# Attention block on one core: row sums taken on TensorE from three running sums, one step less lag, and the last two query blocks kept in the x buffers

## The chip, the cores and the metric

The kernel runs on one core of one Trainium2 chip. The time is the device time of one launch in microseconds (us), the median of several runs. A profile of one execution gives the start and the duration of every instruction. TensorE does matmuls, VectorE (DVE) elementwise work and statistics, ScalarE (ACT) the exponentials, GpSimd (POOL) elementwise work in SBUF, and SyncE (SP) issues most transfers.

## What is computed

```python
# x: (4, 512, 48, 48) float32, so 4 images of 512 channels and t = 2304 positions
hn  = group_norm(x, 32 groups) * gn_scale + gn_bias
qkv = einsum('oc,bchw->bohw', qkv_w, hn) + qkv_b            # fp32 weights
q, k, v = qkv.reshape(b, 3, 8 heads, 64, t).astype(float16)
w   = softmax(einsum('bhct,bhcs->bhts', q * s, k * s))      # s = 1 / 64 ** 0.25
a   = einsum('bhts,bhcs->bhct', w, v)
out = x + einsum('oc,bchw->bohw', proj_w, a) + proj_b
```

The softmax has no maximum subtracted in this path: the exponentials are summed, and the result is divided by the sum. A check of the sums' size sets a flag, and another path would run if it failed.

## The kernel before

Heads go in pairs, one on partitions 0 to 63 and one on 64 to 127; 4 images x 4 pairs are 16 pairs g. Queries go in blocks of 512, 512, 512, 512 and 256 (j = 0 to 4). The 18 groups of 128 keys of a block are worked in steps of three score tiles (BURST); a block of 512 has 6 steps, the block of 256 has 3, so there are 27 x 16 = 432 steps. A step is a unit `u = (g, j, k, last)`.

```python
BURST = 3
BEHIND = 2          # values run this many steps behind the scores

ps_s = ...tile_pool(name="ps_s", bufs=3, space=PSUM)    # score tiles
ps_av = ...tile_pool(name="ps_av", bufs=1, space=PSUM)  # values, and the sums, in turn
ps_w = ...tile_pool(name="ps_w", bufs=1, space=PSUM)    # projections
ppool = ...tile_pool(name="ppool", bufs=3)              # exponentials p of a step

def scores(u):
    pt = ppool.tile([P, BURST, 2, QB], F16, tag="p")
    for r in range(BURST):
        ps = ps_s.tile([P, 2, QB], F32, tag="ps")
        # ... matmuls of both heads into ps ...
        nc.scalar.activation(pt[:, r], ps, AF.Exp)

def values(u):
    # ... av += v^T p for both heads; at the last step of a block:
    if last:
        avx[g, j] = work.tile([P, QB], F32, tag="avx")
        nc.vector.tensor_copy(avx[g, j][:, :n], av[0][:, :n])

def direct(g, j):
    return g == NG - 1 and j >= NQ - 2      # the last two blocks of the last pair

def add(u):
    # ... the first two steps make acc, later ones are added to it (128 x 3072, fp16)
    t = acc[g, j][0]
    nc.vector.tensor_tensor(t, before, pt, ALU.add)
    if last:
        for r in range(1, BURST):           # the join of the three parts
            nc.vector.tensor_tensor(t[:, 0], t[:, 0], t[:, r], ALU.add)
        acc[g, j] = [t[:, :1]]

def add_up(g, j):
    sl = ps_av.tile([P, QB], F32, tag="av")
    steps = [(t, r, a) for t in acc.pop((g, j))
             for r in range(t.shape[1]) for a in range(per)]   # per = 1, or 2 for 256 queries
    for i, (t, r, a) in enumerate(steps):
        for h in range(2):
            lo = h * D
            nc.tensor.matmul(sl[lo : lo + D, :n], ones16, t[:, r, h, a * n : (a + 1) * n],
                             start=(i == 0), stop=(i == len(steps) - 1))
    # ... slx: sl copied to SBUF by VectorE, then transposed by DMA, inverted,
    #     broadcast by DMA (ib), and multiplied into avx by GpSimd, giving att
    # ... for a direct block: reciprocal and product on VectorE instead
```

The output projection of a block converts att to fp32r (`a`), multiplies with a high and a low part of the weights, and adds bias and residual. The residual `r` is loaded from HBM into one of three buffers and becomes the output tile, which is stored from there:

```python
def residual(b, j, m):
    xt = work.tile([P, QB], F32, tag="res", bufs=3)[:, :n]
    nc.sync.dma_start(xt, x[b, bass.ts(m, P), o : o + n])

def att32(b, j, pairs=range(NC)):
    # a buffer of one, "a32", for all four pairs (the very last block: a p buffer)
    for c in pairs:
        engine = nc.vector if direct(b * NPAIR + c, j) else nc.gpsimd
        engine.tensor_copy(at32[b, j][:, c, :n], atts[b * NPAIR + c][:, o : o + n])

def proj_end(b, j, m, ps):
    nc.vector.scalar_tensor_tensor(xt, ps[:, :n], bproj[:, m : m + 1], xt, ALU.add, ALU.add)
    nc.sync.dma_start(out[b, bass.ts(m, P), o : o + n], xt)
```

The loop puts pieces of other work (the next pairs' projections, the next image's statistics, the last image's output projection) between scores and values, by `fill`:

```python
for n in range(end):
    summed = stream[n - BEHIND - 1][:2] if ended(n - BEHIND - 1) else None
    if summed:
        add_up(*summed)
    wanted(stream[n][0], n)
    scores(stream[n])
    if n > 0:
        add(stream[n - 1])
    if summed:
        fill(n)
    if n >= BEHIND:
        values(stream[n - BEHIND])
    # ... check_sums, invert, divide of an ended block, one and two steps later
    if not summed:
        fill(n)
add(stream[-1])
for u in stream[-BEHIND:]:
    values(u)
check_sums(NG - 1, NQ - 2)
att32(B - 1, NQ - 1, range(NC - 1))
add_up(NG - 1, NQ - 1)
att32(B - 1, NQ - 1, (NC - 1,))
while beside:
    issue(end)
# ... the projection of the very last block
```

Of the kernel before, what the change touches and what calls it, by code (L numbers as in the profile page):

```python
# [11 lines left out]
F32 = mybir.dt.float32  # L12
F32R = mybir.dt.float32r
F16 = mybir.dt.float16
I32 = mybir.dt.int32
AF = mybir.ActivationFunctionType
ALU = mybir.AluOpType
# [12 lines left out]
NT = T // P  # L30
SCALE = float(np.float16(1.0 / math.sqrt(math.sqrt(D))))
BURST = 3
BEHIND = 2
LAG = 2


# [430 lines left out]
def fast_path(  # L467
# [169 lines left out]
    def piece(us, run, first=False, last=False, gap=0):  # L637
        return [us, run, first, last, gap, 0, NG]
# [93 lines left out]

    def residual(b, j, m):
        o, n = QBLOCKS[j]
        xt = work.tile([P, QB], F32, tag="res", bufs=3, name=f"r_{b}_{j}_{m}")[:, :n]
        nc.sync.dma_start(xt, x[b, bass.ts(m, P), o : o + n])
        res[b, j, m] = xt

    def att32(b, j, pairs=range(NC)):
        o, n = QBLOCKS[j]  # L740
        if (b, j) == (B - 1, NQ - 1):

            if (b, j) not in at32:
                t = ppool.tile([P, BURST, 2, QB], F16, tag="p", name="a32_last")
                t = t.rearrange("p r h n -> p (r h n)")[:, : 2 * NC * n]
                at32[b, j] = t.bitcast(F32R).rearrange("p (c n) -> p c n", c=NC)
        else:
            at32[b, j] = work.tile(
                [P, NC, QB], F32R, tag="a32", bufs=1, name=f"a32_{b}_{j}"
            )  # L750
        for c in pairs:
            engine = nc.vector if direct(b * NPAIR + c, j) else nc.gpsimd
            engine.tensor_copy(  # L753
                at32[b, j][:, c, :n], atts[b * NPAIR + c][:, o : o + n]
            )

    def proj_chain(b, j, m, ps):
        n = QBLOCKS[j][1]
        for c in range(NC):
            for i, w in enumerate((whi, wlo)):  # L760
                nc.tensor.matmul(  # L761
                    ps[:, :n],
                    w[:, c, bass.ts(m, P)],
                    at32[b, j][:, c, :n],
                    start=(c == 0 and i == 0),
                    stop=(c == NC - 1 and i == 1),
                )
# [9 lines left out]
    def proj_pieces(b, j):  # L777


        n = QBLOCKS[j][1]  # L780

        def run(chunk):
            bank = chain_bank(f"pr_{b}_{j}_{chunk[0]}")
            places = [bank[:, i * n : (i + 1) * n] for i in range(len(chunk))]
            for m, ps in zip(chunk, places):
                proj_chain(b, j, m, ps)
            for m, ps in zip(chunk, places):
                proj_end(b, j, m, ps)

        def ahead(k):  # L790
            if k < NQ * NC:
                residual(b, k // NC, k % NC)

        convert = [piece(0.0, lambda: att32(b, j))]
        chains = []
        per = QB // n
        for m in range(0, NC, per):
            chunk = range(m, m + per)
            loads = [j * NC + i + 2 for i in chunk]
            if (j, m) == (0, 0):  # L800
                loads = [0, 1] + loads
            chains.append(
                [piece(0.0, lambda i=i: ahead(i)) for i in loads]
                + [piece(QB / 290.0, lambda chunk=chunk: run(chunk), True, True)]
            )
        return convert, chains
# [61 lines left out]
    def direct(g, j):  # L868

        return g == NG - 1 and j >= NQ - 2  # L870

    def add(u):

        g, j, k, last = u
        pt = pts[u]
        if k == 0:
            acc[g, j] = [pt]
            return
        if last and direct(g, j):
            acc[g, j].append(pt)  # L880
            return
        before = acc[g, j][0]
        if k == 1:
            acc[g, j] = [
                work.tile(
                    [P, BURST, 2, QB], F16, tag="acc", bufs=1, name=f"acc_{g}_{j}"
                )
            ]
        t = acc[g, j][0]
        nc.vector.tensor_tensor(t, before, pt, ALU.add)  # L890
        if last:
            for r in range(1, BURST):
                nc.vector.tensor_tensor(t[:, 0], t[:, 0], t[:, r], ALU.add)  # L893
            acc[g, j] = [t[:, :1]]

    def add_up(g, j):

        o, n = QBLOCKS[j]
        per = QB // n
        sl = ps_av.tile([P, QB], F32, tag="av", name=f"sl_{g}_{j}")  # L900
        steps = [
            (t, r, a)
            for t in acc.pop((g, j))
            for r in range(t.shape[1])
            for a in range(per)
        ]
        for i, (t, r, a) in enumerate(steps):
            for h in range(2):
                lo = h * D
                nc.tensor.matmul(  # L910
                    sl[lo : lo + D, :n],
                    ones16,
                    t[:, r, h, a * n : (a + 1) * n],
                    start=(i == 0),
                    stop=(i == len(steps) - 1),
                )

        def rows():
            sx = work.tile([P, QB], F32, tag="rows", name=f"slx_{g}_{j}")
            nc.vector.tensor_copy(sx[:, :n], sl[:, :n])  # L920

            sm = small.tile([P, 2, QB // P], F32, tag="sums", name=f"sums_{g}_{j}")
            for h in range(2):
                nc.sync.dma_start(sm[:, h, : n // P], sx[h * D : h * D + 1, :n])
            sums[g, j] = sm
            return sx

        if direct(g, j):
            source = rows() if n == QB else sl
            inv = work.tile([P, QB], F32, tag="rows", name=f"inv_{g}_{j}")  # L930
            nc.vector.reciprocal(inv[:, :n], source[:, :n])
            nc.vector.tensor_tensor(
                atts[g][:, o : o + n], avx.pop((g, j))[:, :n], inv[:, :n], ALU.mult
            )
            if source is sl:
                rows()
        else:
            rows()

    def check_sums(g, j):  # L940
        n = QBLOCKS[j][1]
        sm = sums[g, j][:, :, : n // P]
        ok = fine[:, :, : n // P]
        for op, limit in ((ALU.is_ge, SUM_MIN), (ALU.is_le, SUM_MAX)):
            t = small.tile([P, 2, QB // P], F32, tag="in", name=f"in_{g}_{j}")
            t = t[:, :, : n // P]
            nc.gpsimd.tensor_scalar(t, sm, limit, None, op)  # L947
            nc.gpsimd.tensor_tensor(ok, ok, t, ALU.mult)
# [32 lines left out]
    def put_run(run, *args, gap=0, us=0.0):  # L981

        put([piece(us, lambda: run(*args), us > 0, us > 0, gap)])
# [15 lines left out]

    def ready(b, j):  # L1000

        return BEHIND + (2 if direct((b + 1) * NPAIR - 1, j) else 5)

    def put_convert(b, j):
        end = ends[((b + 1) * NPAIR - 1) * NQ + j]
        put(projs[b, j][0], end + ready(b, j))

    def put_proj(b, j, *which):

        end = ends[((b + 1) * NPAIR - 1) * NQ + j]  # L1010
        for i in which or range(len(projs[b, j][1])):
            put(projs[b, j][1][i], end + ready(b, j) + 1)

    for b in range(B):
# [13 lines left out]
        if b == B - 1:  # L1028
            put_convert(old, 0)
            put_qk(g + 3, 1)  # L1030
            for j in range(NQ):
                put_qk(g + 3, 0, (j,))
                put_proj(old, j)
                if j + 1 < NQ:
                    put_convert(old, j + 1)
            for j in range(NQ - 1):
                put_convert(b, j)
                put_proj(b, j)
            continue

        for j in range(NQ):
# [87 lines left out]
    ended = lambda n: 0 <= n < len(stream) and stream[n][3]  # L1129
    end = len(stream)  # L1130
    for n in range(end):
        summed = stream[n - BEHIND - 1][:2] if ended(n - BEHIND - 1) else None
        if summed:
            add_up(*summed)
        wanted(stream[n][0], n)
        scores(stream[n])
        if n > 0:
            add(stream[n - 1])
        if summed:

            fill(n)
        if n >= BEHIND:
            values(stream[n - BEHIND])
        if ended(n - BEHIND - 2):
            check_sums(*stream[n - BEHIND - 2][:2])
            if not direct(*stream[n - BEHIND - 2][:2]):
                invert(*stream[n - BEHIND - 2][:2])
        if ended(n - BEHIND - 3):
            divide(*stream[n - BEHIND - 3][:2])
        if not summed:  # L1150
            fill(n)
    alone[0] = True
    add(stream[-1])
    for u in stream[-BEHIND:]:
        values(u)
    check_sums(NG - 1, NQ - 2)
    att32(B - 1, NQ - 1, range(NC - 1))
    add_up(NG - 1, NQ - 1)
    att32(B - 1, NQ - 1, (NC - 1,))
    while beside:  # L1160
# [66 lines left out]
```

## Time and profile before

| | |
|---|---|
| time, median of 3 | 1688.02 us (1685.82 to 1689.22) |
| span of the profiled run | 1687.5 us, mean granted TensorE clock 0.987 |
| exponentials, ScalarE | 1296 of 128x1024, mean 1027 ns, 1231.3 us |
| adds of p to the running sums, VectorE | 350 of 128x3072, means 1805 and 1756 ns, 627.6 us |
| transfers of a 128x512 residual / output | 2.9 us / 2.8 us from issue to landing |
| HBM | 47 GB/s over the span |

A line of the profile begins with the line of the kernel and the engine. L893 is the join, L910 the matmuls of the sums, L866 the copy of the values to avx, L890 the adds to the running sums, L832 the scores, L857 the values, L761 the output projection, L772 its eviction, L590 the statistics and L839 the exponentials. PE is TensorE's matmul side and PEld its weight loads. "idle before" is the time that the engine stood still just before, with what ended it behind an arrow.

### The profile page before, as it was taken

How to read it: one execution, taken by the hardware profiler on the slowest of the kernel's cores; microseconds unless marked ns; L12 is line 12 of the kernel's file. 1: busy time of each engine (PE TensorE's matmuls, PEld its weight loads, DVE VectorE, ACT ScalarE, POOL GpSimd, SP SyncE). 2: the span in 40 equal slices, each digit the busy share in tenths (PEclk: the TensorE clock that was granted, in tenths of full speed). 3: DMA queues.
4: the chain of work that ended last, by engine and by line, in shares of the span. 5: the costliest groups of instructions: out<-in, count | busy, mean ns of one | idle time of the engine just before them, and what ended most of it. 6: DMA issues, size and time to landing. Idle time of an engine off the chain costs nothing.

```text
span 1687.5 us, 28311 instructions
## 1 busy us (share of the span) xinstructions
PE 1602.8 (95%) x11504; PEld 702.1 (42%) x11504; DVE 1134.2 (67%) x1280; ACT 1232.6 (73%) x1297; POOL 363.3 (22%) x497
## 2 busy tenths in 40 slices
PE   4999999799999999999999999998999999999796
PEld 1533443244333443445333344444533334444344
DVE  5257666876666667777666666876766666676764
ACT  0078787777787787677777877766777888877980
POOL 1002212112211211232221121133221121223331
PEclk9999999899999999999999999999999999999998
DMA  6001002200000013430100001442110000034243
GB/s 206 1 15 29 13 15 66 70 14 17 14 11 14 17 27 95 128 98 17 48 14 11 14 17 41 102 126 79 22 43 11 14 17 14 14 92 116 58 113 109
DMA packets 93772, 81.84 MB, mean 49 GB/s; under 512 B 50880, under 2 KB 58944, under 8 KB 93632
## 3 DMA queue, kind: packets, MB, share of 16 engines
q1 hardware_dynamic: 91488, 76.51, 17.2%
q10 hardware_dynamic: 1968, 3.41, 0.6%
q8 instruction: 92, 1.51, 0.4%
q14 instruction: 48, 0.39, 0.1%
q0 software_dynamic: 176, 0.02, 0.0%
HBM read 60.44 MB, written 19.16 MB: 47 GB/s over the span
## 4 chain that ended last, share of the span: by engine, by line
PE 86%; DVE 6%; DMA 3%; ACT 3%; issue 2%; POOL 0%; SPq 0%; DVEq 0%; POOLq 0%; ACTq 0%
PE pqk L673 29%; PE ps L832 17%; PE av L857 17%; PE pv L713 14%; PE pr L761 7%; ACT p L839 3%; DVE acc L890 2%; PE sl L910 1%; DVE st L590 1%; DMA out_dram<-r 1%; DMA x<-x_dram 1%; DVE acc L893 1%; DMA r<-x_dram 1%; DVE x L629 0%; DVE r L772 0%
## 5 line engine op out<-in xcount | busy, mean ns | idle before, releaser
L839 ACT ACTIVATE p<-ps 128x1024 f16<-128x1024 f32 x1296 | 1231.3, 1027 | 401.7 <-PE ps L832 400.1
L673 PE MATMUL pqk<-x,wqkv 128*64 128x512 f32 (+1 forms) x2560 | 539.2, 553 | 8.6 <-DVE x L629 4.2
L890 DVE TENSOR_TENSOR acc<-acc,p 128x3072 f16<-128x3072 f16 x270 | 487.2, 1805 | 74.5 <-ACT p L839 74.0
L832 PE MATMUL ps<-q,k 64*128 64x512 f16 (+1 forms) x2880 | 365.7, 361 | 15.6 <-ACT p L839 15.2
L857 PE MATMUL av<-p,v 128*64 128x512 f16 (+1 forms) x2880 | 363.7, 366 | 0.1
L673 PEld LDWEIGHTS pqk<-x,wqkv 128*64 128x64 f32 x2560 | 175.7, 137 | 249.0 <-issue 181.0
L947 POOL TENSOR_SCALAR in<-sums 128x8 f32<-128x8 f32 (+1 forms) x160 | 117.4, 734 | 736.0 <-DMA sums<-slx 728.7
L713 PE MATMUL pv<-wqkv,x 128*64 128x256 f32 x2304 | 267.9, 380 | 2.5 <-DVE r L772 1.5
L832 PEld LDWEIGHTS <-k 64*128 64x128 f16 x2880 | 107.6, 94 | 295.6 <-issue 249.8
L857 PEld LDWEIGHTS <-v 128*64 128x64 f16 x2880 | 132.0, 109 | 212.5 <-issue 169.3
L969 POOL TENSOR_TENSOR att<-avx,ib 128x512 f16<-128x512 f32 (+1 forms) x78 | 125.7, 1612 | 432.1 <-DMA ib<-row 384.6
L713 PEld LDWEIGHTS pv<-wqkv,x 128*64 128x64 f32 x2304 | 159.8, 137 | 96.0 <-DVE v L721 6.4
L890 DVE TENSOR_TENSOR acc<-p,p 128x3072 f16<-128x3072 f16 x80 | 140.4, 1756 | 0.3 <-ACT p L839 0.3
L761 PE MATMUL pr<-a,whi 128*128 128x512 f32 (+1 forms) x304 | 122.8, 410 | 5.6 <-POOL a L753 3.2
L682 DVE TENSOR_SCALAR q<-pqk,bqkv 128x512 f16<-128x512 f32 (+1 forms) x80 | 55.7, 697 | 100.5 <-PE pqk L673 100.2
L721 DVE TENSOR_TENSOR v<-pv,bv 128x512 f16<-128x512 f32 x72 | 49.7, 691 | 103.3 <-PE pv L713 103.2
L893 DVE TENSOR_TENSOR acc<-acc 128x1024 f16<-128x1024 f16 x156 | 112.2, 719 | 5.3
L761 PE MATMUL pr<-a,wlo 128*128 128x512 f32 (+1 forms) x304 | 115.1, 385 | 0.0
L682 DVE TENSOR_SCALAR k<-pqk,bqkv 128x512 f16<-128x512 f32 (+1 forms) x80 | 55.7, 696 | 84.0 <-PE pqk L673 83.9
L772 DVE SCALAR_TENSOR_TENSOR r<-pr,bproj,r 128x512 f32<-128x512 f32 (+1 forms) x80 | 55.3, 695 | 70.3 <-PE pr L761 57.4
L866 DVE COPY avx<-av 128x512 f32<-128x512 f32 (+1 forms) x80 | 50.9, 636 | 57.4 <-PE av L857 57.3
L753 POOL CAST a<-att 128x512 fp32r<-128x512 f16 (+1 forms) x75 | 60.9, 845 | 98.2 <-PE pr L761 97.8
(57 smaller groups left out, 420.8 us busy)
## 6 DMA issues: line engine op xcount, KB each, us to landing
r<-x_dram SPq DMA_DIRECT2D x64, 256.0 KB, 2.9
out_dram<-r SPq DMA_DIRECT2D x64, 256.0 KB, 2.8
ib<-row SPq DMA_DIRECT2D x126, 128.0 KB, 3.0
x<-x_dram SPq DMA_DIRECT2D x56, 256.0 KB, 3.7
x<-x_dram ACTq DMA_DIRECT2D x8, 256.0 KB, 6.8
wqkv<-qkv_wT_dram SPq DMA_DIRECT2D x2, 1024.0 KB, 8.3
sums<-slx SPq DMA_DIRECT2D x128, 2.0 KB, 2.1
r<-x_dram SPq DMA_DIRECT2D x16, 128.0 KB, 2.1
```

What stands on the lines that cost most here:

```text
L673: nc.tensor.matmul(pw[0][lo : lo + D, :n], wqkv[:, c, w0 + lo : w0 + lo + D], hn[b, c, j], start=(c == 0), stop=(c == NC - 1),)
L682: nc.vector.tensor_scalar(qk[g][part][:, o : o + n], pw[0][:, :n], bqkv[:, col : col + 1], SCALE, ALU.add, ALU.mult,)
L713: nc.tensor.matmul(pw[0][lo : lo + D, a, :], hn[b, c, i * P // QB][:, at + lo : at + lo + D], wqkv[:, c, 2 * C + half * C // 2 :][:, : C / ...
L753: engine.tensor_copy(at32[b, j][:, c, :n], atts[b * NPAIR + c][:, o : o + n])
L761: nc.tensor.matmul(ps[:, :n], w[:, c, bass.ts(m, P)], at32[b, j][:, c, :n], start=(c == 0 and i == 0), stop=(c == NC - 1 and i == 1),)
L832: nc.tensor.matmul(ps[:, h, a * n : (a + 1) * n], kt[rows, bass.ts(i, P)], qt[rows, o : o + n], start=True, stop=True,)
L839: nc.scalar.activation(pt[:, r], ps, AF.Exp)
L857: nc.tensor.matmul(av[0][lo : lo + D, :n], vv[b, pr // 2][:, i, pr % 2 * P + lo : pr % 2 * P + lo + D], pt[:, r, h, a * n : (a + 1) * n], ...
L890: nc.vector.tensor_tensor(t, before, pt, ALU.add)
L893: nc.vector.tensor_tensor(t[:, 0], t[:, 0], t[:, r], ALU.add)
L947: nc.gpsimd.tensor_scalar(t, sm, limit, None, op)
L969: nc.gpsimd.tensor_tensor(atts[g][:, o : o + n], avx.pop((g, j))[:, :n], ib[:, :n], ALU.mult)
```

## The change

Three things change together. The join of the three parts of a running sum on VectorE is left out, and the sum matmuls on TensorE take all three parts. Values run one step behind the scores instead of two, and all that follows an ended block comes a step earlier. And the residuals and the converted att of the last two query blocks go to the x buffers, which nobody reads any more in the last pair; they are loaded and converted (three of four pairs) during the last pair, so that the end need not wait for three residual buffers in turn.

```diff
-BEHIND = 2
...
     def residual(b, j, m):
         o, n = QBLOCKS[j]
-        xt = work.tile([P, QB], F32, tag="res", bufs=3, name=f"r_{b}_{j}_{m}")[:, :n]
+        if at_end(b, j):
+
+            tag = f"x{m}_{j - NQ + 2}"
+            xt = xpool.tile([P, QB], F32, tag=tag, name=f"r_{b}_{j}_{m}")[:, :n]
+        else:
+            xt = work.tile([P, QB], F32, tag="res", bufs=3, name=f"r_{b}_{j}_{m}")
+            xt = xt[:, :n]
         nc.sync.dma_start(xt, x[b, bass.ts(m, P), o : o + n])
...
+    def at_end(b, j):
+
+        return b == B - 1 and j >= NQ - 2
...
-        if (b, j) == (B - 1, NQ - 1):
-            (cut: a p buffer for the last block; one a32 buffer for all pairs else)
+        if (b, j) not in at32:
+            if at_end(b, j):
+                at32[b, j] = [
+                    xpool.tile([P, n], F32R, tag=f"x{c}_{j}", name=f"a32_{b}_{j}_{c}")
+                    for c in range(NC)
+                ]
...
-        convert = [piece(0.0, lambda: att32(b, j))]
+        convert = [
+            piece(0.0, lambda: att32(b, j, (NC - 1,) if at_end(b, j) else range(NC)))
+        ]
...
-        t = acc[g, j][0]
-        nc.vector.tensor_tensor(t, before, pt, ALU.add)
-        if last:
-            for r in range(1, BURST):
-                nc.vector.tensor_tensor(t[:, 0], t[:, 0], t[:, r], ALU.add)
-            acc[g, j] = [t[:, :1]]
+        nc.vector.tensor_tensor(acc[g, j][0], before, pt, ALU.add)
...
-            for r in range(t.shape[1])
+            for r in range(BURST)
...
-        return BEHIND + (2 if direct((b + 1) * NPAIR - 1, j) else 5)
+        return 3 if direct((b + 1) * NPAIR - 1, j) else 6
...
-            for j in range(NQ - 1):
+            for j in range(NQ - 2):
                 put_convert(b, j)
                 put_proj(b, j)
+                if j < 2:
+                    for m in range(NC):
+                        put_run(residual, b, NQ - 2 + j, m)
+                    put_run(att32, b, NQ - 2 + j, range(NC - 1))
+            put_convert(b, NQ - 2)
+            put_proj(b, NQ - 2)
             continue
...
     for n in range(end):
-        summed = stream[n - BEHIND - 1][:2] if ended(n - BEHIND - 1) else None
-        if summed:
-            add_up(*summed)
+        if ended(n - 2):
+            add_up(*stream[n - 2][:2])
         wanted(stream[n][0], n)
         scores(stream[n])
         if n > 0:
             add(stream[n - 1])
-        if summed:
+        if ended(n - 2):
 
             fill(n)
-        if n >= BEHIND:
-            values(stream[n - BEHIND])
+        if n > 0:
+            values(stream[n - 1])
...
     alone[0] = True
     add(stream[-1])
-    for u in stream[-BEHIND:]:
-        values(u)
-    check_sums(NG - 1, NQ - 2)
-    att32(B - 1, NQ - 1, range(NC - 1))
+    values(stream[-1])
     add_up(NG - 1, NQ - 1)
     att32(B - 1, NQ - 1, (NC - 1,))
```

More of the change, by code (lines that the diff above doesn't have):

```diff
@@ L734, in residual @@
         o, n = QBLOCKS[j]
-        xt = work.tile([P, QB], F32, tag="res", bufs=3, name=f"r_{b}_{j}_{m}")[:, :n]
+        if at_end(b, j):
[4 more added lines that the diff above has]
+            xt = xt[:, :n]
         nc.sync.dma_start(xt, x[b, bass.ts(m, P), o : o + n])
         res[b, j, m] = xt
+    def at_end(b, j):
+        return b == B - 1 and j >= NQ - 2
     def att32(b, j, pairs=range(NC)):
         o, n = QBLOCKS[j]
-        if (b, j) == (B - 1, NQ - 1):
[L743 to L750, printed above, removed]
+        if (b, j) not in at32:
[4 more added lines that the diff above has]
+                ]
+            else:
+                t = work.tile(
+                    [P, NC, QB], F32R, tag="a32", bufs=1, name=f"a32_{b}_{j}"
+                )
+                at32[b, j] = [t[:, c, :n] for c in range(NC)]
         for c in pairs:
             engine = nc.vector if direct(b * NPAIR + c, j) else nc.gpsimd
-            engine.tensor_copy(
-                at32[b, j][:, c, :n], atts[b * NPAIR + c][:, o : o + n]
-            )
+            engine.tensor_copy(at32[b, j][c], atts[b * NPAIR + c][:, o : o + n])
     def proj_chain(b, j, m, ps):
@@ L763, in proj_chain @@
                     w[:, c, bass.ts(m, P)],
-                    at32[b, j][:, c, :n],
+                    at32[b, j][c],
                     start=(c == 0 and i == 0),
@@ L790, in ahead @@
         def ahead(k):
-            if k < NQ * NC:
+            if k < NQ * NC and not at_end(b, k // NC):
                 residual(b, k // NC, k % NC)
-        convert = [piece(0.0, lambda: att32(b, j))]
+        convert = [
+            piece(0.0, lambda: att32(b, j, (NC - 1,) if at_end(b, j) else range(NC)))
+        ]
         chains = []
@@ L1138, in fast_path @@
             add(stream[n - 1])
-        if summed:
+        if ended(n - 2):
             fill(n)
-        if n >= BEHIND:
-            values(stream[n - BEHIND])
[L1144 to L1150, printed above, removed]
+        if n > 0:
+            values(stream[n - 1])
+        if ended(n - 3):
+            check_sums(*stream[n - 3][:2])
+            if not direct(*stream[n - 3][:2]):
+                invert(*stream[n - 3][:2])
+        if ended(n - 4):
+            divide(*stream[n - 4][:2])
+        if not ended(n - 2):
             fill(n)
```

## The prediction

> **What bounds the kernel now.** I read the page's engine shares first, then the groups, then the span in stretches, and last the chain and the timeline where the stretches were not full.
>
> ```profile
> PE 1602.8 (95%) x11504; PEld 702.1 (42%) x11504; DVE 1134.2 (67%) x1280; ACT 1232.6 (73%) x1297; POOL 363.3 (22%) x497
> ```
>
> TensorE is busy 95% of the span. A share is an average, so here is the span in stretches of 50 us (columns: window, length, then busy time and count of PE, weight loads, VectorE, ScalarE, GpSimd, then granted clock, DMA share, GB/s).
>
> ```profile
> 250.00:300.00 50.00, 50.00 (x370) 19.64 (x370) 32.96 (x36) 40.02 (x43) 10.23 (x15) 1.00 0.32 77
> 300.00:350.00 50.00, 39.49 (x278) 15.44 (x276) 43.12 (x65) 36.09 (x39) 9.90 (x13) 0.90 0.16 44
> ...
> 1300.00:1350.00 50.00, 50.00 (x326) 17.21 (x324) 34.29 (x35) 42.19 (x45) 8.24 (x10) 1.00 0.06 12
> ...
> 1550.00:1600.00 50.00, 41.85 (x310) 19.89 (x309) 36.15 (x37) 44.75 (x49) 16.37 (x23) 0.97 0.29 76
> 1600.00:1650.00 50.00, 45.32 (x288) 22.95 (x287) 32.98 (x32) 40.74 (x44) 15.16 (x19) 1.00 0.37 101
> 1650.00:1700.00 50.00, 20.67 (x136) 16.74 (x130) 14.22 (x22) 0.00 (x0) 5.15 (x14) 0.85 0.27 86
> ```
>
> Most stretches look like 250 or 1300: TensorE is full to the last tenth and VectorE has a third of its time free. There an instruction added to TensorE is paid, and one taken from VectorE earns nothing. The exceptions are few. At 300 to 350 (and, milder, near 700 and 1100) the statistics of the next image sit on VectorE, and TensorE waits for it. From 1550 to 1650, the last pair, there is no query, key or value projection left to fill in, and the exponentials set the pace. After 1650 comes a tail of 37.5 us with TensorE 20.67 us busy.
>
> The groups concerned (columns: line, engine, operation, tiles, shapes, count, then busy us and mean ns, then idle before it):
>
> ```profile
> L893 DVE TENSOR_TENSOR acc<-acc 128x1024 f16<-128x1024 f16 x156 | 112.2, 719 | 5.3
> L910 PE MATMUL sl<-acc,ones 128*64 128x512 f16 x132 | 26.1, 395 | 7.8 <-DVE avx L866 7.8
> L910 PE MATMUL sl<-acc,ones 128*64 128x256 f16 x72 | 7.3, 297 | 3.3 <-DVE avx L866 3.3
> ```
>
> The joins are 112.2 us of VectorE. What matters is how much of that the chain that ended last runs through. Its by-line heading gives them 0.8% of 1687.5 us, and its pieces, listed over the whole span, add up to 13.0 us, all near the statistics. An example:
>
> ```profile
> 324.45 0.99 DVE acc L893
> ...
> 326.07 2.46 DVE st L590 x4
> 328.54 0.59 DVE avx L866
> ```
>
> The column sums (sl) cannot start before avx has left the shared PSUM bank, and avx stands behind the joins and the statistics. So TensorE waits.
>
> The price of the sum matmuls is best read where twelve stand in a row, because a mean of pipelined matmuls overstates them. These are the timeline's rows of TensorE near the end (start us, duration, idle before in brackets):
>
> ```profile
> 1645.18 0.84 PE L910 MATMUL sl<-acc,ones 128*64 128x512 f16 x6
> 1645.86 0.81 PE L910 MATMUL sl<-p,ones 128*64 128x512 f16 x6
> 1646.60 0.83 PE L832 MATMUL ps<-q,k 64*128 64x256 f16 x12
> ...
> 1649.42 2.16 PE L857 MATMUL av<-p,v 128*64 128x256 f16 x36
> ...
> 1654.29 1.48 PE L910 MATMUL sl<-acc,ones 128*64 128x256 f16 x12 [2.71 <-DVE avx L866]
> ```
>
> From start to start, twelve of 512 columns take 1.42 us, 0.118 each; thirty-six of 256 take 2.16, 0.060 each. The last row also shows a wait of 2.71 us in the tail.
>
> **What the Trainium skill says.** "TensorE: Matmul & The Clock Gate", section "Part 3: Packing small matmuls — row/col tiling": matmuls in distinct column groups run concurrently. The two heads' sums write partitions 0 to 63 and 64 to 127, and the trace agrees: 0.237 us for a pair, about what the section "Back-to-back issue gap" of that page gives for one of 512 columns (0.216). Same page, "Part 1: The HAM clock gate": TensorE idle for about 3.4 us falls to half clock. The trace agrees: after the wait of 4.90 us before 329.18 the granted clock is 0.66 over 330 to 340, and six score matmuls take 1.46 us where they took 0.82. "SBUF — State Buffer", section "Who interferes with whom": a VectorE instruction with two SBUF inputs contends with GpSimd reads. It agrees: two adds take 4.48 us at 319.93, beside a GpSimd multiplication, where one alone takes 1.75. Joins are of that kind too, so the few on the chain are partly the stretched ones.
>
> **The change part by part.**
>
> *Sums on TensorE, added.* A block of 512 queries goes from 2 sum matmuls to 6, one of 256 queries from 4 to 12. The last two blocks of the last pair never had a join and stay. So 63 blocks x 4 x 0.118 = 29.7 us and 15 blocks x 8 x 0.060 = 7.2 us: 36.9 us (372 matmuls). Three of these blocks lie in the last pair, where ScalarE sets the pace: minus 1.4. Near the statistics and where the first projections wait for a transfer some three more are hidden: minus 1.5. Paid: about +34 us.
>
> *Joins off VectorE.* 112.2 us of work goes, 13.0 us of it on the chain. What stood next behind each (adds, statistics, TensorE's own queue) takes part of the room; I choose two thirds: -8.5 us.
>
> *One step less lag.* Values of a step now follow the scores of the next one, not of the second next. Score tiles are three deep and a step has three, so the last score of a step already waits for the previous step's last exponential; the values behind it find their operand ready. I expect no new wait in the body. Both orders free a p buffer in time. At the end it pulls the last blocks' sums one step forward: a step in the last pair is 2.75 us (1637.45 to 1640.36 and on), in which TensorE mostly waited.
>
> *The tail.* Count from the start of the second last block's sums, 1645.18, to the end: 42.3 us now. In the new order TensorE has: those sums 1.42, scores 0.76, a projection chain 2.06, values 0.72, scores 0.76, values 0.72, a chain 2.06, values 0.72: 9.2. Then a wait of 0.9 for avx (VectorE is free now, since the long reciprocal of 3.35 us came a step earlier), the last sums 24 x 0.060 = 1.4, one chain 2.1, four chains 7.9 (1662.05 to 1669.99 today) and the small ones 4.0 (to 1673.95): 25.5. Residuals are in SBUF by then, so two evictions of 0.48 us and their start follow at once, 1.2, and the 7.2 us that today lie between the last eviction (1680.31) and the end: 33.9. That is 8.4 less. Today the last four evictions trail TensorE by 6.4 us because each waits for its residual to land, and a chain waits for conversions on GpSimd; both go. With the step above: -11 us.
>
> Sum: 1688 + 34 - 8.5 - 11 = 1702.5; I say 1702.
>
> **The rivals.** *The added matmuls are hidden, and only the gains remain.* They would be if VectorE or ScalarE set the pace; the time would be near 1669. The final pair and the statistics stretches speak for it, the full stretches at 250 and 1300 against it: TensorE's idle time between 100 and 1550 us is some 30 us in all, in a few places.
>
> *VectorE's relief is worth much more.* Each stall also drops the clock, so 13 us of joins could drag some more behind them: near 1690. Against it: the stall at 320 to 334 is mostly adds and statistics (29.9% and 21.1% of the chain there) and these stay.
>
> *The shorter lag makes TensorE wait.* Values now depend on exponentials one step old, and avx has one add ahead of it on VectorE, which can be late; the sums then wait behind avx. Were that 0.3 us in each of 80 blocks, it is 24 us: near 1726. Against it: avx stood behind an add of its own step in the old order too, and a filler of 1.9 to 2.1 us stands between values and sums in both.
>
> *The tail gives nothing*, because the output transfers end it anyway: near 1711. Against it: the residual waits in it are plain in the trace.
>
> **Range and chances.** The large term, +34, is worked out from counts and in-place durations; I trust it to 5 us. The tail could be 5 to 13, the joins 3 to 13, and the lag is one-sided upward. So 1690 to 1714, with 1702 in it. A gain over 2% (below 1654) would need the sums free and more beside it: 0.01. A loss over 2% (above 1722) needs the lag to cost 20 us: 0.05. Within 2%: 0.94.
>
> **What would show it.** In the new profile the sum matmuls should be 594, and in the chain a block's sums about 0.66 to 0.7 us where they were 0.22; joins absent and VectorE near 1025 us; TensorE busy near 1630 and the full stretches still full; no residual transfer in the chain after the last exponential, and about 26 us from the last exponential's end to the end of the span, where they are 37.5 (1649.95 to 1687.5) now: 33.9 less the 4.96 before the last scores and the 3.35 from those to the end of their exponentials. The prediction is wrong if ScalarE's wait for scores or the sums' wait for avx grows (lag), or if the pairs of sum matmuls cost much more than 0.24 us between other work.

## The result, and the profile after

The changed kernel takes 1705.78 us (1704.47 to 1708.84) against 1688.62 us for the kernel before, measured beside it: a ratio of 1.0105, 95% interval 1.0084 to 1.0126. It is 17 us slower, and 3.8 us above the predicted 1702.

The page's engine shares after:

```profile
PE 1630.7 (96%) x11876; PEld 720.4 (42%) x11876; DVE 1018.7 (60%) x1124; ACT 1232.9 (72%) x1297; POOL 347.0 (20%) x497
```

VectorE has lost 115 us, and TensorE has gained 372 matmuls. The same stretches as before the change (busy time and count of PE, weight loads, VectorE, ScalarE, GpSimd, then clock, DMA share, GB/s):

```profile
250.00:300.00 50.00, 50.00 (x392) 21.08 (x386) 27.95 (x29) 39.00 (x42) 9.52 (x15) 1.00 0.23 58
300.00:350.00 50.00, 42.04 (x282) 15.45 (x282) 40.38 (x60) 37.44 (x40) 11.00 (x13) 0.93 0.25 63
...
1300.00:1350.00 50.00, 50.00 (x328) 17.25 (x326) 27.90 (x27) 39.14 (x43) 11.42 (x14) 1.00 0.05 9
```

TensorE is as full as it was at 250 and 1300, and VectorE went from 33 and 34 us there to 28: time freed where nobody waited for it. The stretch with the statistics is a little fuller than before (42.04 us busy for 39.49).

The chain that ended last, in an ordinary stretch of the changed kernel (start, us, what):

```profile
454.75 0.86 PE pqk L672 x4
455.61 0.65 PE sl L915 x6
456.26 0.75 PE ps L842 x6
457.01 1.88 PE pqk L672 x16
```

The chain stays on TensorE, and a block's sums are now 0.65 us in it, where two matmuls were 0.22. That is 0.43 us a block. The groups of the sums:

```profile
L915 PE MATMUL sl<-acc,ones 128*64 128x512 f16 x384 | 54.2, 389 | 12.5 <-DVE avx L876 12.3
L915 PE MATMUL sl<-acc,ones 128*64 128x256 f16 x192 | 13.2, 273 | 0.5 <-DVE avx L876 0.5
```

And the end, in the chain:

```profile
1680.13 0.80 PE av L867 x12
...
1680.95 0.44 DVE avx L876
...
1681.43 1.51 PE sl L915 x24
...
1686.77 10.11 PE pr L769 x58
...
1696.91 0.88 DVE r L780 x2
```

No residual is waited for any more. The wait for avx before the last sums is 0.52 us instead of 2.71, and the two last evictions follow TensorE at once.

A ruler for what follows: the exponentials are the same 1296 instructions in the same order in every kernel here, 81 to a pair of heads. The start of each 81st in the timeline gives the length of a pair.

| us | before | after |
|---|---|---|
| second pair (nothing but TensorE limits it) | 94.06 | 96.24 |
| ninth pair (the same) | 95.62 | 97.78 |
| last pair | 86.07 | 89.93 |
| first to last exponential | 1558.66 | 1585.32 |
| last exponential's start to the end | 38.57 | 26.10 |

### The profile page after: what moved, and what is told of

It is laid out like the page before. It is cut to its first block, busy times and chain, and to the rows that moved or that the text cites. A ratio compares the mean times of both kernels' runs of the same rounds, so it can differ in the third digit from the quotient of the medians.

```text
span 1704.3 us, 28889 instructions
## 1 busy us (share of the span) xinstructions
PE 1630.7 (96%) x11876; PEld 720.4 (42%) x11876; DVE 1018.7 (60%) x1124; ACT 1232.9 (72%) x1297; POOL 347.0 (20%) x497
## 3 DMA queue, kind: packets, MB, share of 16 engines
q1 hardware_dynamic: 91488, 76.51, 16.4%
## 4 chain that ended last, share of the span: by engine, by line
PE 88%; DVE 5%; DMA 3%; ACT 3%; issue 2%; POOL 0%; SPq 0%; ACTq 0%; DVEq 0%; POOLq 0%
PE pqk L672 29%; PE ps L842 17%; PE av L867 17%; PE pv L712 14%; PE pr L769 7%; PE sl L915 3%; ACT p L849 3%; DVE acc L899 2%; DMA out_dram<-r 1%; DVE st L589 1%; DMA x<-x_dram 1%; DVE x L628 1%; DVE avx L876 0%; DVE inv L936 0%; DMA r<-x_dram 0%
## 5 line engine op out<-in xcount | busy, mean ns | idle before, releaser
L899 DVE TENSOR_TENSOR acc<-acc,p 128x3072 f16<-128x3072 f16 x270 | 481.9, 1785 | 81.8 <-ACT p L849 81.1
L952 POOL TENSOR_SCALAR in<-sums 128x8 f32<-128x8 f32 (+1 forms) x160 | 113.8, 711 | 806.6 <-DMA sums<-slx 800.1
L763 POOL CAST a<-att 128x512 fp32r<-128x512 f16 (+1 forms) x78 | 65.2, 870 | 84.2 <-PE pr L769 83.7
L915 PE MATMUL sl<-acc,ones 128*64 128x512 f16 (+1 forms) x576 | 67.4, 350 | 13.0 <-DVE avx L876 12.8
L769 PEld LDWEIGHTS pr<-a,whi 128*128 128x128 f32 x320 | 60.4, 189 | 41.2 <-issue 21.9
```

Of the source, the lines that this page charges most:

```text
L763: engine.tensor_copy(at32[b, j][c], atts[b * NPAIR + c][:, o : o + n])
L769: nc.tensor.matmul(ps[:, :n], w[:, c, bass.ts(m, P)], at32[b, j][c], start=(c == 0 and i == 0), stop=(c == NC - 1 and i == 1),)
L899: nc.vector.tensor_tensor(acc[g, j][0], before, pt, ALU.add)
```

## The experiments

Three things changed together, so I took them one at a time and in pairs. "Join" is the join on VectorE, the lag is 1 or 2 steps, and "x" says that the last two blocks live in the x buffers.

| kernel | join | lag | end | us | ratio to before, 95% |
|---|---|---|---|---|---|
| before | yes | 2 | three buffers | 1685.37 | |
| nojoin_lag2_res | no | 2 | three buffers | 1701.67 | 1.0096 (1.0072 to 1.0120) |
| nojoin_lag2_x | no | 2 | x | 1699.52 | 1.0074 (1.0047 to 1.0101) |
| changed kernel | no | 1 | x | 1705.78 | 1.0105 (1.0084 to 1.0126) |
| join_lag2_x | yes | 2 | x | 1678.39 | 0.9953 (0.9934 to 0.9972) |
| join_lag1_x | yes | 1 | x | 1761.90 | 1.0454 (1.0429 to 1.0479) |

(The kernel before was 1688.62 beside the changed kernel's first measurement, and 1685.37 beside the others. The ratios come from all runs of both kernels and can differ by 0.001 from the quotient of the medians.)

**The sums alone.** The kernel before without its joins:

```diff
-        t = acc[g, j][0]
-        nc.vector.tensor_tensor(t, before, pt, ALU.add)
-        if last:
-            for r in range(1, BURST):
-                nc.vector.tensor_tensor(t[:, 0], t[:, 0], t[:, r], ALU.add)
-            acc[g, j] = [t[:, :1]]
+        nc.vector.tensor_tensor(acc[g, j][0], before, pt, ALU.add)
```

> The kernel before with the joins alone taken out, sums on TensorE; lag of two steps, residuals in three buffers. Theory: the sums' part alone, 34 less 9, so 1711 to 1716. Rival (the lag carries a part of the loss): 1695 to 1705.

It took 1701.67 us, 16 more than the kernel before and some 10 less than the theory said, inside the range that I had given to the rival. The trace says which term is off. The second and the ninth pair are 2.17 us longer (96.23 and 97.79), so the price of the matmuls is 0.434 us a block, and 78 blocks cost 33.9. Between the first and the last exponential the kernel is only 17.5 us longer (1576.18). So leaving out the joins gave back 16.4 us in these two traces, where I had counted 11.4 (8.5 for the joins, 2.9 for matmuls that would be hidden). The other pairs of kernels that differ in the joins alone, with a lag of two and the x buffers, give 16 to 17 by their traces and 13 to 15 by their medians.

**The price of a matmul.** Each of the block's sum matmuls done twice with weights of one half, which gives the same sums:

```diff
+            for _ in range(1 if direct(g, j) else 2)
...
-                    ones16,
+                    ones16 if direct(g, j) else half16,
```

> No joins, lag of two steps, x buffers, and each of a block's sum matmuls done twice with weights of one half, so 12 (or 24) instead of 6 (or 12) in 78 blocks. Theory (TensorE is full and each 512 column matmul costs 0.108 us, 0.65 a block): 3.2 us more in an undisturbed pair of heads, 45 to 50 us in all, 1.034 to 1.038 of the kernel before. Rival (the cost of the sums is a wait or a switch per block and not the matmuls): less than 15 us more, below 1.017.

1750.56 us, 1.0394 (1.0369 to 1.0418), 51 us above its base, nojoin_lag2_x, which was measured on another chip. The second pair grew from 96.23 to 99.47, by 3.24, as expected. In the chain:

```profile
466.61 1.29 PE sl L919 x12
```

Twelve matmuls in 1.29 us where six take 0.65: the cost is the matmuls themselves, 0.108 us each for 512 columns, and no switch or wait of a block. The total and the ratio are a little above what was expected (45 to 50 us, 1.034 to 1.038).

**The x buffers alone.**

```diff
-        xt = work.tile([P, QB], F32, tag="res", bufs=3, name=f"r_{b}_{j}_{m}")[:, :n]
+        if at_end(b, j):
+            tag = f"x{m}_{j - NQ + 2}"
+            xt = xpool.tile([P, QB], F32, tag=tag, name=f"r_{b}_{j}_{m}")[:, :n]
...   (and the converted att of these blocks, as in the change)
```

> The kernel before with the last two blocks' residuals and converted att in the x buffers alone; joins and a lag of two steps kept. Theory (of the 11 us of the tail the x buffers carry 8.4 and the shorter lag 2.75): 1679 to 1682, some 2 to 3 us above the same with a lag of one. Rival (the tail is shorter because of the shorter lag, the transfers being hidden anyway): within 3 us of the kernel before, 1686 to 1690.

1678.39 us, 7.0 below the kernel before; the theory holds, with a slightly smaller number. From the last exponential to the end it is 31.11 us instead of 38.57, 7.5 less. The expectation's last words, that a lag of one would be 2 to 3 us better still, fell with the run join_lag1_x, below.

Residuals alone, without the conversions:

> The kernel before with the last two blocks' residuals alone in the x buffers, their att converted as before. Theory (the tail waits for residuals to land): most of the 7 us that residuals and conversions together gave, ratio 0.995 to 0.9975. Rival (the tail waits for the conversions on GpSimd): less than 2 us, 0.9985 to 1.

1680.14 us, 0.9971 (0.9962 to 0.9980): 5.2 of the 7 us. The tail is 32.70 us. The conversions on GpSimd still hold TensorE up in it, as the timeline of that run shows:

```profile
1661.17 0.50 PE L771 MATMUL pr<-a,whi 128*128 128x512 f32 x1 [0.74 <-POOL a L763]
```

**The joins put back into the changed kernel.** The same lines as in the first diff, the other way round.

> The changed kernel with the joins on VectorE put back, so that a block's sums take 2 (256 queries: 4) matmuls again; lag of one step and x buffers as in the changed kernel. Theory (sums cost 34 us on TensorE, joins 9 us on the path, lag nothing in the body, tail 11): the time falls to 1677 to 1682, below both kernels, undisturbed pairs fall by 2.2 us each. Rival (the lag of one step makes TensorE wait for values or for avx in each block): it stays at 1690 or above, because the waits stay when the matmuls go.

1761.90 us, 83 us above join_lag2_x, and far from the 1677 to 1682 that I expected. My account of the lag was wrong, and the rival is right that TensorE waits for avx before the sums. But the wait did not merely stay when the matmuls went: it grew with the joins, from the changed kernel's 12.8 us (shown further on). The wait in this run, then in join_lag2_x (us in total, times, longest):

```profile
PE sl L920 <- DVE avx L876: 83.8, 71, 4.3
```

```profile
PE sl L921 <- DVE avx L877: 11.1, 7, 4.9
```

An ordinary block in the timeline shows the race:

```profile
209.53 1.76 DVE L900 TENSOR_TENSOR acc<-acc,p 128x3072 f16<-128x3072 f16 x1 [1.05 <-ACT p L849]
209.89 2.86 ACT L849 ACTIVATE p<-ps 128x1024 f16<-128x1024 f32 x3 [0.39 <-PE ps L842]
210.21 0.84 PE L867 MATMUL av<-p,v 128*64 128x512 f16 x6
210.88 1.89 PE L712 MATMUL pv<-wqkv,x 128*64 128x256 f32 x16
211.32 1.42 DVE L903 TENSOR_TENSOR acc<-acc 128x1024 f16<-128x1024 f16 x2
212.65 0.68 DVE L876 COPY avx<-av 128x512 f32<-128x512 f32 x1
...
213.39 0.41 PE L920 MATMUL sl<-acc,ones 128*64 128x512 f16 x2 [0.62 <-DVE avx L876]
```

With a lag of one the block's last add, its joins and avx are due in one step. VectorE comes to avx only at 212.65, and TensorE, which was done with its filler 0.62 us before the sums could start, stands still. With a lag of two the last add and the joins have a step of their own. The step in which avx falls then is the first of the next block, and a block's first step has no add (its p is only kept for the second). The same place in join_lag2_x:

```profile
209.15 1.42 DVE L904 TENSOR_TENSOR acc<-acc 128x1024 f16<-128x1024 f16 x2
...
212.61 0.69 DVE L877 COPY avx<-av 128x512 f32<-128x512 f32 x1 [1.26 <-PE av L868]
...
213.69 0.38 PE L921 MATMUL sl<-acc,ones 128*64 128x512 f16 x2
```

VectorE has been idle for 1.26 us when the values are ready for avx, and the sums follow without a wait. So the joins and the lag belong together. Taking out the joins is what makes a lag of one bearable at all.

**Half the joins.** One join put back instead of two:

```diff
-            for r in range(1, BURST):
-                nc.vector.tensor_tensor(t[:, 0], t[:, 0], t[:, r], ALU.add)
-            acc[g, j] = [t[:, :1]]
+            nc.vector.tensor_tensor(t[:, 0], t[:, 0], t[:, 2], ALU.add)
+            acc[g, j] = [t[:, :2]]
```

> The changed kernel (lag of one, x buffers) with one join of the two put back, 0.7 us of VectorE a block, and sums of 4 (or 8) matmuls. Theory (with a lag of one, avx stands behind the block's last add and its joins, TensorE reaches the sums about 0.1 us before avx is out without joins, and 1.4 us of joins push it past): not half way between 1706 and 1762 but near the changed kernel, 1.01 to 1.025 of the kernel before. Rival (each join costs its own length in each block): half way, 1.025 to 1.03 or above.

1722.72 us, 1.0224 (1.0201 to 1.0247), in the theory's range but near its upper end, where the rival begins. Its wait:

```profile
PE sl L919 <- DVE avx L876: 36.2, 45, 3.4
```

A join of 0.7 us in each of 78 blocks is 55 us of VectorE. The first raises the wait by 23 us (12.8 to 36.2), the second by 48 (to 83.8). So the slack of a block hides a good part of the first join and little of the second; the threshold is there, but not sharp.

**The lag without joins.** The rows of the changed kernel and of nojoin_lag2_x stood some 5 us apart by their ratios, measured on different chips, so both were measured once more side by side.

> The changed kernel once more, beside its twin with a lag of two on the same chip, because the two were measured on different chips so far (1.0105 and 1.0074, intervals that overlap). Theory (the shorter lag costs 6 us near the statistics and gives 2 in the last pair and the tail): 3 to 5 us above the twin. Rival (the lag is free without joins, and the difference was the chip): within 1.5 us of the twin.

> The changed kernel with a lag of two steps instead of one: no joins, x buffers. Theory: 1706 to 1710, above the changed kernel by the 2.75 us of one step at the end. Rival (a lag of one costs 0.3 us in each of 80 blocks): about 1685, below the changed kernel by 20 us or more.

> The twin with a lag of two steps. Theory: 1.007 to 1.0085 of the kernel before, 3 to 5 us below the changed kernel. Rival: equal to the changed kernel within 1.5 us.

nojoin_lag2_x gave 1.0074 and, repeated, 1697.11 us, 1.0073 (1.0057 to 1.0088). The changed kernel repeated is 1707.60 us, 1.0120 (1.0100 to 1.0141): 10.5 us above its twin by the medians, 8 by the ratios. No expectation met this: nojoin_lag2_x was to lie above the changed kernel, or 20 us and more below it, and the repeated runs were to lie 3 to 5 us apart, or within 1.5. First to last exponential the lag of one costs 10.2 us in the first two traces and 16.2 in the second two (1585.32 to 1575.07, 1588.30 to 1572.09), of which 3.0 and 2.1 lie in the last pair; from the last exponential to the end it gives 5.0 and 5.1. The waits of the changed kernel and of nojoin_lag2_x for avx, the same to a tenth in the repeated traces:

```profile
PE sl L915 <- DVE avx L876: 12.8, 10, 2.7
```

```profile
PE sl L916 <- DVE avx L877: 7.3, 4, 3.1
```

An example of the difference in the chain of the changed kernel:

```profile
670.42 1.27 DVE st L589 x2
671.69 1.66 DVE acc L899
673.35 0.61 DVE avx L876
...
674.00 0.84 PE sl L915 x6
```

Where the statistics have made VectorE late, add and avx stand in a row before the sums. Between the first exponential and the last pair this wait is 11.0 us with a lag of one, against 3.1 and 3.2 with two. So it accounts for the whole of the 7.2 us that the lag costs there in the first two traces, and for 8 of the 14.1 in the second two. Of the rest, some 5 us is TensorE being busy longer with the same work: in the seventh pair the same 706 matmuls keep it busy for 102.4 us at a mean granted clock of 0.95, against 98.3 us at 1.00.

The largest single loss is the seventh pair's second block, 22.8 us with a lag of two and 29.1 and 31.8 with one. The chain of the changed kernel, run again, goes there through the division of a block:

```profile
717.41 2.90 DMA row<-inv
...
721.51 3.54 DMA ib<-row
...
725.21 2.40 POOL att L974
727.61 0.56 POOL a L763
...
728.22 2.93 PE pr L769 x6
```

The projection waits for att, att for its reciprocal's way through memory. That this comes from the earlier place of the projection is argued from the chain; no run tried it alone. It is also more a shift than a loss: over the stretch before the last pair TensorE waits for `a` as long with a lag of two (3.6 and 4.1 us, in the eleventh pair) as with one (3.3 and 4.6, mostly in the seventh), and the eleventh pair is 3.6 and 2.4 us shorter with a lag of one.

**Where the joins hurt.** The joins of join_lag2_x left out in 12 of 78 blocks, those near the statistics, chosen from the lengths of the blocks in the traces with and without joins:

```diff
+UNJOINED = {(0, 1), (2, 0), (2, 1), (2, 3), (5, 3), (5, 4), (6, 0), (7, 0), (10, 0), (10, 1), (10, 2), (10, 3)}
...
-        if last:
+        if last and (g, j) not in UNJOINED:
```

> Joins kept, lag of two steps, x buffers; the join is left out in 12 of 78 blocks, those whose neighbours hold the statistics of the next image on VectorE, and there the sums take 6 (or 12) matmuls. Theory (the joins cost time only where the statistics keep VectorE late, the added matmuls cost 0.43 us everywhere else): about 9 us below the kernel with all joins and x buffers, ratio to the kernel before 0.989 to 0.992. Rival (what leaving out joins gave is spread thinly over all blocks): at most 2 us below it, 0.994 to 0.997.

1672.95 us, 0.9924 (0.9905 to 0.9943), 5.4 below join_lag2_x, which was measured on another chip: between theory and rival. So both were measured once more.

> Joins, lag of two, x buffers, once more as the neighbour of the next. Theory: 0.995 to 0.996 of the kernel before.

> The same without the join in the 12 blocks near the statistics. Its trace showed 10.7 us less between the first and the last exponential than the run with all joins, its times only 5. Theory (trace): 8 to 11 us below its neighbour. Rival (times; the neighbour's profiled execution had a stall that most of its executions don't have): 4 to 6 us below.

1678.43 us (0.9957, 0.9942 to 0.9973) and 1673.72 us (0.9924, 0.9904 to 0.9945): 4.7 apart, so the second expectation's rival is right and the 10.7 us of the first pair of traces were partly one execution's scatter: between the first and last exponential join_lag2_x took 1558.59 us in one profiled execution and 1554.36 in the other, join_some_lag2_x 1547.89 and 1552.38, so the second pair of traces is only 2.0 apart. By the medians leaving out the join gives some 5 us net in these 12 blocks, which is 10 us less 12 times 0.43 for the matmuls. Leaving it out in the other 66 blocks too (nojoin_lag2_x) then costs 23 to 27 us, 0.35 to 0.40 a block. So nearly the full price of the matmuls is paid there, and the joins gain little: most of what leaving out joins gives lies in the 12 blocks. This version is the fastest of all here, 12 us below the kernel before and 33 below the changed one.

## Why the prediction was right or wrong

The number was right, but partly by luck: two terms were off in opposite directions, and one of them had the wrong sign.

*Sums on TensorE.* Predicted 0.47 us a block, 36.9 in all; measured 0.43 and 33.9, 0.108 us a matmul of 512 columns in place of 0.118. The mean taken from twelve in a row near the end was slightly high. The "minus 1.4" for blocks of the last pair was wrong in kind: with a lag of two each of its three blocks costs 0.43 us too. The third block's sums, for instance, fall into the fourth block's exponentials, which take 20.77 us without joins and 20.33 with them. Sums stand ahead of the next scores, and ScalarE waits for scores there (1.65 us at 1642.93 in nojoin_lag2_x), so a matmul before them is paid although TensorE has idle time elsewhere in the step.

*Joins off VectorE.* The term was mis-sized: "I choose two thirds: -8.5", with 2.9 more for hidden matmuls; measured 16.4 in place of these 11.4, and 13 to 17 in the other comparisons. That is as much as the 13.0 us of joins on the chain or more, so the rival that stalls drag something behind them had a point, of a few us. (The shares that I held against it, 29.9% and 21.1%, are those of 320 to 340 us, not of 320 to 334.) From the first exponential to the last pair TensorE's idle time falls by 10.1 us without joins (30.4 to 20.3, nojoin_lag2_res against the kernel before). Its busy time grows by 26.8 (1442.2 to 1469.0), where the sums of the 74 blocks in it add 32. The missing 5 us are matmuls that take less time; the mean granted clock rises from 0.987 to 0.992, so I put it down to the clock, which is argued. Not every stall is gone: in nojoin_lag2_x the clock still falls to 0.56 over 330 to 340 us.

*One step less lag.* The step that failed is "I expect no new wait in the body". I compared scores, exponentials and values and found the operands ready, which they are. The wait is one further on: avx has to leave the shared PSUM bank before the sums, it stands behind the block's last add on VectorE, and with a lag of one both are due in the same step. The third rival said just this, and I set it aside with two arguments. The first, that "avx stood behind an add of its own step in the old order too", is false: with a lag of two, avx falls into the first step of the next block, which has no add, so the old order gave VectorE a whole step of slack that the new one takes away. The second was a filler of 1.9 to 2.1 us that would cover the add. It does cover an add and avx in an ordinary block (0.0 to 0.1 us lost), but not where statistics have made VectorE late: 7 and 14 us in the body outside the last pair, in the two pairs of traces, 8 us in each by the wait for avx. Two joins more, and it costs 83 us. The gain of 2.75 us at the end was there: 5.0 less in the tail, 2 to 3 more in the last pair. (The two times that the prediction gives for a step, 1637.45 and 1640.36, lie 2.91 apart, not 2.75.)

*The tail.* From the start of the second last block's sums to the end 33.9 us were predicted and 33.4 measured (1670.90 to 1704.3); from the last exponential's end to the end of the span 26 and 25.1. The x buffers' part was 7.0 to 7.3 us with joins (8.4 predicted), and most of it is the residuals.

So the sum in the prediction, +34 - 8.5 - 11, was in truth about +34 less 13 to 17 for sums and joins, 2 to 7 down for the x buffers (2.2 by the medians and 3.7 by the ratios of the two kernels without joins, 7 with them), and 5 to 10 up for the lag. The joins gave 2 to 6 us more than predicted, the x buffers 1 to 6 less, and the lag took 5 to 10 where it was to give 2.75; that these cancel in good part is luck. What it said to look for came true: 594 sum matmuls, 0.65 us for a block's sums, VectorE at 1018.7 us (1025 predicted), TensorE busy for 1630.7 us, full stretches still full. So did its sign of error: the sums' wait for avx grew, from 11.1 us to 12.8 although the joins were gone, and by its own words that makes its account of the lag wrong.

## What to carry to other kernels

Where one engine is full, work moved onto it is paid at its streaming price, and work taken off another pays back mostly in the stretches in which that other is late, as these runs show it for TensorE and VectorE; so choose by stretch, as the version that keeps most joins does. A software lag is the slack of every engine that works between producer and consumer: before shortening it, add up all that the slowest of these has to do in one step, with the buffer's release at the end, and not only whether the operands are ready. And take a change of three parts apart before judging it: here one part (the x buffers) was worth 7 us and was buried under the others.

## What was not expected of the hardware

Stretches without a stall repeat to a hundredth of a microsecond: the tenth pair took 97.95 to 97.96 us in all five profiled executions without joins and with single sums, on at least two chips and with both lags. In the two traces of the changed kernel nine of the sixteen pairs agree to 0.03 us. The others, among them the three in which TensorE waits for the statistics, differ by up to 2.8, so the scatter of 3 to 9 us between executions sits in them or ahead of the first exponential. So a change of a few tenths of a microsecond in an ordinary block can be read from one trace, where whole times would need many runs.
